# Router scores of a mixture-of-depths stage: from DVE sums over token rows to TensorE products over channel rows

## The chip, the cores and the metric

The kernel runs on one core of a Trainium2 chip, as one program. The metric is the device time in microseconds, the median of three runs. All arithmetic is float32.

The engines by the profile's names: PE (TensorE, matrix products; PEld is its weight load), DVE (VectorE), ACT (ScalarE), POOL (GpSimd), and SP, which issues most DMAs. Each engine takes its instructions in the order in which the program wrote them.

## The reference, cut to what matters

An image of 2 x 256 x 56 x 56 goes through a convolution with local attention, a positional term, six Mamba layers, and then a tail on tokens (2 batches of 3136 tokens of 256 channels). The edit is in the first stage of the tail, a feed-forward layer that only the better half of the tokens of a batch goes through:

```python
t = t + _L2_ffn_ref(_ln_t(t), ...)          # x = _ln_t(t): layer norm of each token
weights = (einsum('bsd,do->bso', x, wr) + br)[..., 0]
_, idx = top_k(weights, k)                  # k = s // 2; the last of them is dropped
h = gelu(sel @ w1 + b1);  y = (h @ w2 + b2) * w_sel
processed = zeros_like(x).at[idx].set(y);  return processed + x
```

The score of a token is one number: the normalised token times the vector `wr`, plus `br`. With mean m and scale r of the token, that is r * (sum(t * wr) - m * sum(wr)) + br, so only sum(t * wr) needs the 256 channels. Behind this stage come an attention step over the two batches and a mixture of eight experts.

## The kernel before, in words

The tail (`tail_phase`, from line 1260) works in groups of 448 tokens, as four rows of 112 (`TK`): seven groups g in each of two batches b. The batch's tokens lie in `t[b]`, 112 partitions by 28 by 256.

The order on each engine is written by a small planner, `Flow`. Each step of work is a Python generator. It takes a tile from a named pool (`yield take("mid")`), waits for a flag (`need`), or says which engine it has just used and for how long by estimate (`yield "PE", 1.1`). The planner resumes generators by these estimates, and the instructions fall into each engine's queue in that order. Another estimate, or another tile, thus moves instructions on all engines. Pools that matter here: `turn` and `mid`, three PSUM tiles each; `chan`, four tiles of channel rows (128 channels by 2 by 448 tokens); `rows`, token rows.

`prepare(b, g)` (line 1404) is the edited generator. It takes the group's channel rows x (for batch 0 from `head[g]`, for batch 1 by a DMA into a `chan` tile), transposes them on PE (L1421) and copies them to `t[b]` on ACT (L1338). `norm` (L1358 to L1367) makes mean and variance on DVE, the root on POOL (L1364), and the two derived columns `up` and `off` on DVE. Then four DVE instructions (L1438) multiply each token row with `wr`, which lies in all 112 partitions, and add it up into `score`; L1444 to L1448 finish the scores. Their product rows go to a `rows` tile that nobody reads; after them ACT writes the normalised rows into the same tile (L1452) and SP stores it to `x_d` (L1457). The generator holds that tile from before L1438.

Batch 0's seven groups run together, with `rest()`, the last step of the Mamba phase: y products (L821, L825) on PE, squares (ACT L776, PE L780), a root (ACT L788, L789), its spread (PE L795), the weighting (DVE L803), an addition on POOL (L845) and a store (SP L846). Four loads of batch 1's channel rows (L1468) stand on SP behind all of these. Batch 1's groups start one after the other: each waits until the one before is scored.

`select(0)` starts when batch 0 is scored. Two radix searches of four rounds each find the threshold: DVE compares and counts (L1534 to L1539), PE adds over the partitions (L1522). Prefix sums follow (L1553, L1554), and `invert` turns places into a list of tokens with one-hots (DVE L1583 to L1591, in `chan` tiles) and products (PE L1596), which ends in `pick` (DVE L1662). POOL gathers the rows by this list (L1396), PE transposes them (L1348), and `dense` runs the two layers (PE L1702, ACT L1708, PE L1716), with `mid` tiles for the first. `select(1)` and `dense(1)` follow.

Of the kernel before, what the change touches and what calls it, by code (L numbers as in the profile page):

```python
# [16 lines left out]
ALU = mybir.AluOpType  # L17
# [4 lines left out]
P = 128  # L22
# [23 lines left out]
TK = 112  # L46
# [13 lines left out]
def chunk(c, n=NT):  # L60
    return slice(c * n, (c + 1) * n)
# [1198 lines left out]
def tail_phase(ctx: ExitStack, tc: tile.TileContext, I, t2_d, out, rest):  # L1260
# [6 lines left out]
    nc = tc.nc  # L1267
# [7 lines left out]
    flow = Flow()  # L1275

    def fixed(shape, name, dtype=F32):
        return cp.tile(shape, dtype, name=name)

    def load(shape, name, src):  # L1280
        t = fixed(shape, name)
        nc.sync.dma_start(t, src)
        return t
# [14 lines left out]
    def take(name):  # L1298
        return "take", name

    def need(*flag):
        return "need", flag
# [6 lines left out]
    wr = load([TK, C], "wr", I["wr_row"].unsqueeze(0).to_broadcast([TK, C]))  # L1309
    earlier = load([TK, TK], "earlier", I["earlier"])  # L1310
    places = load([TK, P], "places", I["count"].unsqueeze(0).to_broadcast([TK, P]))
    token = load([TK, NTK], "token", I["token"])
    wr_sum = fixed([TK, 1], "wr_sum")
    nc.vector.tensor_reduce(wr_sum, wr, AX.X, ALU.add)
    st = [fixed([TK, 6], f"st{n}") for n in range(8)]
# [7 lines left out]
    t, mv, rs, up, off, score = [], [], [], [], [], []  # L1323
# [9 lines left out]
    def four(g):  # L1333
        return slice(4 * g, 4 * g + 4)

    def move(which, dst, src):
        if which == "ACT":
            nc.scalar.copy(dst, src)  # L1338
        else:
            nc.vector.tensor_copy(dst, src)  # L1340
        return which, 0.65
# [11 lines left out]
    def norm(b, g):  # L1353

        s = four(g)
        for n in range(4 * g, 4 * g + 4, 2):
            for i in range(n, n + 2):
                nc.vector.bn_stats(st[i % 8], t[b][:, i, :])  # L1358
            for i in range(n, n + 2):
                nc.vector.bn_aggr(mv[b][:, i, :], st[i % 8])  # L1360
            yield "DVE", 1.1
        nc.vector.tensor_scalar(rs[b][:, s], mv[b][:, s, 1], 1e-5, 0.0, ALU.add, ALU.add)
        yield "DVE", 0.2
        nc.gpsimd.tensor_tensor(rs[b][:, s], rs[b][:, s], half.to_broadcast([TK, 4]), ALU.pow)  # L1364
        yield "POOL", 1.1
        nc.vector.tensor_scalar(up[b][:, s], rs[b][:, s], 1.0, 0.0, ALU.add, ALU.add)
        nc.vector.scalar_tensor_tensor(  # L1367
            off[b][:, s], mv[b][:, s, 0], -1.0, rs[b][:, s], ALU.mult, ALU.mult
        )
# [22 lines left out]
    def rows_of(d, b, g):  # L1392
        return d[b][chunk(g, GT), :].rearrange("(n p) c -> p n c", p=TK)
# [10 lines left out]
    def prepare(b, g):  # L1404

        if b == 0:
            x = head[g]
        else:
            yield need("prepared", 0, NG - 1)
            if g:  # L1410
                yield need("scored", 1, g - 1)
            x = early.pop(g, None)
            if x is None:
                x = yield take("chan")
                nc.sync.dma_start(x, t2_v[b, :, :, chunk(g, GT)])
                yield "wait", 4.0
        for n in range(2):
            ps = yield take("turn")
            for i in range(2):
                for k in range(2):  # L1420
                    nc.tensor.transpose(  # L1421
                        ps[:TK, i * C + k * P : i * C + k * P + P],
                        x[:, k, chunk(2 * n + i, TK)], ident,
                    )
            yield "PE", 0.8
            yield move(
                "ACT", t[b][:, 4 * g + 2 * n : 4 * g + 2 * n + 2, :],
                ps[:TK].rearrange("p (n c) -> p n c", c=C),
            )
            flow.give("turn", ps)  # L1430
        if b:
            flow.give("chan", x)
        yield from norm(b, g)
        s = four(g)
        x = yield take("rows")
        for n in range(0, 4, 2):
            for i in range(4 * g + n, 4 * g + n + 2):
                nc.vector.scalar_tensor_tensor(  # L1438
                    x[:TK, i % 4, :], t[b][:, i, :], 1.0, wr, ALU.mult, ALU.mult,
                    accum_out=score[b][:, i : i + 1],  # L1440
                )
            yield "DVE", 1.1
        sc = score[b][:, s]
        nc.vector.scalar_tensor_tensor(  # L1444
            sc, mv[b][:, s, 0], wr_sum, sc, ALU.mult, ALU.subtract
        )
        nc.vector.scalar_tensor_tensor(sc, sc, -1.0, rs[b][:, s], ALU.mult, ALU.mult)
        nc.vector.tensor_scalar(sc, sc, vec[:TK, V_BR : V_BR + 1], 0.0, ALU.add, ALU.add)  # L1448
        yield "DVE", 0.5
        flow.done("scored", b, g)  # L1450
        for n, i in enumerate(range(4 * g, 4 * g + 4)):
            nc.scalar.activation(  # L1452
                x[:TK, n, :], t[b][:, i, :], AF.Identity,
                scale=rs[b][:, i : i + 1], bias=off[b][:, i : i + 1],
            )
        yield "ACT", 2.4
        nc.sync.dma_start(rows_of(x_d, b, g), x[:TK])  # L1457
        yield "wait", 2.5
        flow.give("rows", x)
        flow.done("prepared", b, g)  # L1460

    flow.start(rest, *[prepare(0, g) for g in range(NG)])
    flow.run()
    cp = pool("tl_const")
# [699 lines left out]
    for b in range(B):  # L2164
        if b:
            flow.start(*[prepare(b, g) for g in range(NG)])
        else:
            flow.start(weights())
        flow.start(select(b), dispatch(b))
# [134 lines left out]
```

## Time and profile before

| what | value |
| --- | --- |
| median of three runs | 8828.61 us (8826.25 to 8833.44) |
| profiled execution | 8834.56 us |
| its span, first to last instruction | 8832.8 us |
| mean granted PE clock | 0.97 |
| busy share: PE, DVE, ACT, POOL | 84%, 89%, 75%, 86% |
| batch 0 prepared | about 7909 to 7956 us of the span |
| L1438, the sums of the scores | 56 instructions, 0.42 us in the median |
| the tail, from its first loads | 7906 to 8833 us |

The busy shares are those of the whole span, of which nine tenths are the convolution and the Mamba layers. The tail is another program in effect, and its stages have limits of their own, so they are read by stretches of the span. In a line of the timeline the first number is the start, the second the length in microseconds; the brackets hold the idle time of that engine before it and what ended it. In a stretch's line each engine has its busy time and, in parentheses, its number of instructions; then come the granted PE clock, the share of the DMA engines, and GB/s.

### The profile page before, as it was taken

The page shows a single profiled execution, that of the slowest core. Times are in us where ns is not written, and L with a number is a line of the kernel's source. Part 1 is how long each engine was busy: PE and PEld are TensorE (multiplying, and loading weights), DVE is VectorE, ACT ScalarE, POOL GpSimd, SP SyncE. Part 2 cuts the span into 40 slices and gives each one's busy share as a digit, 9 for nine tenths or more (in the row PEclk, how much of TensorE's full clock was granted, in tenths as well). Part 3 has the DMA queues.
Part 4 walks back from the last instruction along what each step waited for, and adds up shares of the span by engine and source line. Part 5 has one row for each costly group of instructions (what it writes and reads, how often), then busy time and mean ns, then how long its engine had stood idle before and what let it go on. Part 6 is the DMA issues. An engine that isn't in the chain of part 4 may idle for free.

```text
span 8832.8 us, 106454 instructions
## 1 busy us (share of the span) xinstructions
PE 7458.7 (84%) x32350; PEld 3282.6 (37%) x32350; DVE 7845.9 (89%) x7140; ACT 6659.6 (75%) x15914; POOL 7609.8 (86%) x5255
## 2 busy tenths in 40 slices
PE   9988888888888888888888888888888888867987
PEld 6553333333333333333333333333333333325776
DVE  3339999999999999999999999999999999985664
ACT  1238888888888888888888888888888888863432
POOL 2339999999999999999999999999999999982354
PEclk9999999999999999999999999999999999988988
DMA  2335565655656555556566565556556565543225
GB/s 85 100 116 127 135 135 126 136 131 132 135 132 133 131 132 135 134 133 148 136 137 137 127 133 134 130 133 135 130 133 134 127 138 130 134 118 93 65 72 150
DMA packets 698246, 1118.31 MB, mean 127 GB/s; under 512 B 80060, under 2 KB 675843, under 8 KB 697667
## 3 DMA queue, kind: packets, MB, share of 16 engines
q1 hardware_dynamic: 682888, 1072.49, 52.5%
q0 software_dynamic: 14784, 39.01, 1.5%
q8 instruction: 257, 4.21, 0.2%
q14 instruction: 317, 2.60, 0.1%
HBM read 892.62 MB, written 218.60 MB: 126 GB/s over the span
## 4 chain that ended last, share of the span: by engine, by line
PE 44%; ACT 33%; DVE 13%; issue 6%; DMA 2%; POOL 2%; SPq 0%; ACTq 0%; DVEq 0%; POOLq 0%
ACT da L896 12%; PE mm L683 9%; PE mm L665 8%; PE mm L821 6%; DVE da L934 4%; PE acc L949 4%; DVE x L934 4%; ACT dt L742 2%; DVE x L926 2%; ACT dt L750 2%; ACT hz L695 2%; PE mm L754 2%; ACT dt L749 2%; ACT hz L700 2%; ACT dt L758 1%
## 5 line engine op out<-in xcount | busy, mean ns | idle before, releaser
L913 POOL TENSOR_TENSOR x<-dtur,bc 128x900 f32<-128x900 f32 x2688 | 4717.0, 1793 | 7.8 <-DMA dtur<-dtu_d 7.6
L896 ACT ACTIVATE da<-dtr,am 128x451 f32<-128x451 f32 x5376 | 3417.0, 641 | 323.7 <-DVE x L934 153.9
L934 DVE TENSOR_TENSOR_SCAN da<-da,x 128x902 f32<-128x902 f32 x1512 | 3040.1, 2031 | 97.5 <-ACT da L896 70.9
L934 DVE TENSOR_TENSOR_SCAN x<-da,x 128x902 f32<-128x902 f32 x1176 | 2341.5, 2018 | 46.6 <-ACT da L896 38.2
L926 POOL TENSOR_TENSOR x<-x,bc 128x896 f32<-128x896 f32 x1176 | 2080.1, 1784 | 80.9 <-DVE x L934 80.9
L926 DVE TENSOR_TENSOR x<-da,bc 128x896 f32<-128x896 f32 x1512 | 1604.1, 1075 | 20.5 <-ACT state L922 9.0
L949 PE MATMUL acc<-x,sum_w 128*32 128x448 f32 x10752 | 1382.5, 568 | 59.2 <-DVE x L926 33.9
L683 PE MATMUL mm<-u,w_cv 128*128 128x448 f32 x2656 | 1093.8, 554 | 67.0 <-ACT tail L678 56.9
L665 PE MATMUL mm<-xn,w_z 128*128 128x448 f32 x1328 | 587.0, 564 | 196.5 <-ACT dt L758 116.7
L683 PEld LDWEIGHTS mm<-u,w_cv 128*128 128x128 f32 x2656 | 478.6, 190 | 677.7 <-issue 375.9
L665 PE MATMUL mm<-xn,w_u 128*128 128x448 f32 x1328 | 579.0, 558 | 121.2 <-ACT hz L695 111.8
L821 PE MATMUL mm<-hz,w_out 128*128 128x448 f32 x1344 | 553.7, 555 | 107.9 <-ACT tail L678 56.3
L949 PEld LDWEIGHTS acc<-x,sum_w 128*32 128x32 f32 x10752 | 266.2, 111 | 966.7 <-issue 732.7
L754 PE MATMUL mm<-dt,mb_ident 128*128 128x448 f32 x666 | 342.1, 595 | 257.6 <-ACT state L922 139.4
L737 PE MATMUL mm<-xd,w_dt 128*128 128x448 f32 x664 | 339.2, 592 | 217.2 <-ACT dtu L745 128.6
L912 ACT COPY x<-state 128x2 f32<-128x2 f32 x2688 | 437.1, 187 | 0.1
L665 PEld LDWEIGHTS mm<-xn,w_z 128*128 128x128 f32 x1328 | 225.4, 189 | 564.5 <-ACT dt L758 236.4
L665 PEld LDWEIGHTS mm<-xn,w_u 128*128 128x128 f32 x1328 | 231.5, 189 | 457.8 <-ACT hz L695 223.1
L821 PEld LDWEIGHTS mm<-hz,w_out 128*128 128x128 f32 x1344 | 243.3, 191 | 417.9 <-issue 189.2
L766 POOL TENSOR_TENSOR dtu<-dt,hz 128x448 f32<-128x448 f32 x336 | 330.9, 985 | 76.6 <-PE mm L755 76.6
L695 ACT ACTIVATE hz<-mm,vec 128x448 f32<-128x448 f32 x332 | 209.2, 630 | 243.1 <-PE mm L683 238.8
L944 PE MATMUL acc<-hz,w_sk 128*128 128x448 f32 x672 | 347.0, 600 | 31.7 <-DVE hz L963 31.7
(377 smaller groups left out, 9536.9 us busy)
## 6 DMA issues: line engine op xcount, KB each, us to landing
dtr<-dt_d SPq DMA_DIRECT2D x1344, 224.0 KB, 4.4
dtur<-dtu_d SPq DMA_DIRECT2D x1344, 224.0 KB, 6.7
bc<-bc_d SPq DMA_DIRECT2D x336, 448.0 KB, 7.8
dt_d<-dt SPq DMA_DIRECT2D x336, 224.0 KB, 6.2
dtu_d<-dtu SPq DMA_DIRECT2D x336, 224.0 KB, 2.0
rows<-r_d SPq DMA_DIRECT2D x28, 448.0 KB, 7.9
xg<-in_x SPq DMA_DIRECT2D x26, 448.0 KB, 8.9
bm<-in_edge SPq DMA_DIRECT2D x16, 539.0 KB, 4.6
```

Source lines behind the costliest of these rows:

```text
L665: nc.tensor.matmul(ps, lhsT=w[:, k, chunk(d, P)], rhs=Q["xn"][:, k, :], start=(k == 0), stop=(k == 1),)
L683: nc.tensor.matmul(ps, lhsT=w_cv[:, 4 * d + k, :], rhs=M["u", d][:, k : k + T], start=(k == 0), stop=(k == 3),)
L695: nc.scalar.activation(hz(j)[:, d, :], M["mm"], AF.Identity, bias=layer_of(j + 1)["cb"][:, d : d + 1])
L754: nc.tensor.matmul(ps, lhsT=ident, rhs=M["dt"][:, d, :], start=True, stop=False)
L821: nc.tensor.matmul(ps, lhsT=layer_of(j - 1)["w_out"][:, d, chunk(k, P)], rhs=gated(j - 1)[:, d, :], start=(d == 0), stop=False,)
L896: nc.scalar.activation(D[i][:, chunk(g, R)], dtr[:, 2 * pr + g, :], AF.Exp, scale=L["am"][:, col : col + 1],)
L912: nc.scalar.copy(x[:, :, 0:1], states(i))
L913: nc.gpsimd.tensor_tensor(x[:, :, 1:], Q[k][1][:, 2 * pr : 2 * pr + 2, :], wide(Q["bc"][:, ng, :]), ALU.mult)
L926: engine.tensor_tensor(both(X[i])[:, :, 1 : T + 1], both(h)[:, :, 1 : T + 1], wide(QS[j]["bc"][:, 4 + ng, :T]), ALU.mult,)
L934: nc.vector.tensor_tensor_scan(h, D[i], X[i], 0.0, ALU.mult, ALU.add)
L944: nc.tensor.matmul(acc[0][:, :T], lhsT=L["w_sk"][:, k, :], rhs=Q["hz"][:, k, :], start=True, stop=False,)
L949: nc.tensor.matmul(acc[0][chunk(g, HD), :T], lhsT=sum_w, rhs=both(X[i - 1 + g // 2])[:, g % 2, 1 : T + 1], start=False, stop=(ng == 3), ti ...
```

## The change

The sum over channels is taken on PE from the channel rows, before they are given back, instead of on DVE from the token rows. `wr` is loaded a second time, as two columns of 128 channels. For each row of 112 tokens two products (the two halves of the channels) add up one column of a `mid` tile, eight products a group; L1444 reads it from there. The `mid` tile is held from the products until L1444, through `norm`. A `chan` tile is held until the products are issued. The `rows` tile is taken only after the scores. The planner's estimates change with it: 1.1 for PE is new, two of 1.1 for DVE are gone.

```diff
+    wr_col = fixed([P, 2], "wr_col")
+    nc.sync.dma_start(wr_col, I["wr_row"].rearrange("(k p) -> p k", p=P))
...
             flow.give("turn", ps)
+        raw = yield take("mid")
+        for i in range(4):
+            for k in range(2):
+                nc.tensor.matmul(
+                    raw[:TK, i : i + 1], lhsT=x[:, k, chunk(i, TK)], rhs=wr_col[:, k : k + 1],
+                    start=(k == 0), stop=(k == 1),
+                )
+        yield "PE", 1.1
         if b:
             flow.give("chan", x)
         yield from norm(b, g)
         s = four(g)
-        x = yield take("rows")
-        for n in range(0, 4, 2):
-            for i in range(4 * g + n, 4 * g + n + 2):
-                nc.vector.scalar_tensor_tensor(
-                    x[:TK, i % 4, :], t[b][:, i, :], 1.0, wr, ALU.mult, ALU.mult,
-                    accum_out=score[b][:, i : i + 1],
-                )
-            yield "DVE", 1.1
         sc = score[b][:, s]
         nc.vector.scalar_tensor_tensor(
-            sc, mv[b][:, s, 0], wr_sum, sc, ALU.mult, ALU.subtract
-        )
+            sc, mv[b][:, s, 0], wr_sum, raw[:TK, :4], ALU.mult, ALU.subtract
+        )
+        flow.give("mid", raw)
         nc.vector.scalar_tensor_tensor(sc, sc, -1.0, rs[b][:, s], ALU.mult, ALU.mult)
         nc.vector.tensor_scalar(sc, sc, vec[:TK, V_BR : V_BR + 1], 0.0, ALU.add, ALU.add)
         yield "DVE", 0.5
         flow.done("scored", b, g)
+        x = yield take("rows")
```

## The prediction

> **What bounds the kernel now.** I read the page first, then the busy time by stretch around the edited stage, the edited line by itself, the timeline and the chain of waits there. Times of the walk are given less 7900 us.
>
> ```profile
> span 8832.8 us, 106454 instructions
> ```
>
> ```profile
> 7931.00:7938.00 7.00, 5.19 (x42) 4.28 (x40) 7.00 (x43) 5.95 (x13) 2.45 (x3) 1.00 0.00 0
> 7938.00:7956.00 18.00, 0.00 (x0) 0.00 (x0) 17.44 (x95) 12.10 (x24) 7.37 (x10) 0.51 0.55 167
> 7956.00:7998.00 42.00, 12.66 (x53) 10.34 (x54) 32.48 (x152) 7.89 (x15) 2.02 (x2) 0.50 0.59 193
> 7998.00:8011.00 13.00, 12.28 (x64) 12.07 (x64) 8.15 (x33) 3.25 (x6) 1.67 (x1) 0.50 0.24 71
> 8020.00:8060.00 40.00, 40.00 (x168) 27.61 (x169) 18.07 (x83) 19.14 (x34) 11.84 (x12) 0.96 0.32 94
> ```
>
> The columns are PE, weight loads, DVE, ACT, POOL, then the granted clock. Nothing before 7908 is touched. Batch 0 is scored between 7920 and 7956, and there DVE is full. `select(0)` runs from 7956 to 8011, a relay of short DVE and PE steps. From 8020 PE is full, 40.00 of 40 us, so DVE time taken away there is worth nothing and PE time added costs its full length. Last, the clock: it falls to half at 38.2 and stays there to 8022, also in 7998 to 8011, where PE is busy 12.28 of 13 us.
>
> ```profile
> L1438 DVE SCALAR_TENSOR_TENSOR rows<-t,wr x56: 412/418/1635, 7932.2 to 8057.2; 112x256 f32<-112x256 f32 x56
> ```
>
> ```profile
> 537.49 3.15 PE L780 MATMUL early<-mb_mean_w,sq 128*112 128x1 f32 x16 [3.66 <-ACT sq L776]
> ```
>
> ```profile
> 8171.54 1.64 PE L1789 MATMUL mid<-vec,query 128*112 128x1 f32 x16
> ```
>
> The first line is what goes: 56 DVE sums, 0.35 us from start to start where they stand in a row (7932.17, 7932.51, 7932.86 in the timeline). The two others are the shape that comes (eight 128x112 by 128x1 products, recorded as 16): 3.1 us at half clock and, its first weight load left out, 1.5 us at full.
>
> ```profile
> 7930.41 3.04 POOL L1364 TENSOR_TENSOR rs<-rs,tl_half 112x4 f32<-112x4 f32 x3 [19.99 <-DVE rs L1362]
> ...
> 7935.50 1.14 PE L795 MATMUL mm<-mb_ident,rss 112*128 112x112 f32 x8
> ...
> 7939.59 1.24 DVE L803 SCALAR_TENSOR_TENSOR o<-res,normf,mm 128x448 f32<-128x448 f32 x2
> 7940.91 2.07 POOL L845 TENSOR_TENSOR hz<-hz,o 128x896 f32<-128x896 f32 x1 [1.02 <-DVE o L803]
> ```
>
> ```profile
> 7956.61 4.98 DMA chan<-t_d
> 7961.64 1.12 PE turn L1421 x4
> ...
> 8003.69 2.80 PE mid L1596 x14
> 8006.48 1.77 PE turn L1421 x8
> 8008.26 2.46 PE mid L1596 x14
> 8010.75 0.17 DVE pick L1662
> ```
>
> The four timeline lines are the last step of `rest()`, threaded through batch 0: its L795 feeds L803, that feeds POOL's L845. The chain shows what follows batch 0: SP may issue the loads of batch 1 only after the last `x_d` store, which waits for ACT's last L1452 (ends 56.2); then the relay; then `pick`, after which rows are gathered and PE's full stretch starts.
>
> **The change part by part.** Removed: 56 x 0.35 = 19.6 us of DVE, half in each batch. In batch 1 the last three groups' share lies beside a full PE and was worth nothing. Added: 14 x 16 recorded products, 1.5 or 3.1 us a group. The written order of the engines moves too, and it decides. I lay the new order out with these durations.
>
> *Batch 0.* PE leaves `rest()`'s second L825 at 31.4. The new order then has products of g0, transposes, g1, transposes, g2, transposes (3 x 1.5 + 3 x 0.5): 37.4. L780 follows, during which the clock falls (38.2): 39.6. Transposes at half clock 1.1: 40.7. Then the products of g3, g4 and g5 stand ahead of L795: 3 x 3.1, so 50.0, and L795 ends about 52.0 against 36.6. They find their PSUM tiles free in time (DVE's first three scores end by 37.8).
> DVE has L803 ahead of the `rs` step of g3 in the new order, so DVE stands still at it from about 41.3, and all behind it waits: L803 ends 53.2. POOL has L845 ahead of the L1364 steps of g3 to g6; before, g3's came ahead of it and DVE fed the others in time: L845 ends 55.3, then L1364 of g3, g4, g5 at 1.0 us each. ACT's L1452 needs these: four groups from 56.6 at 2.07 us each end at 64.9, against 56.2. So +8.7 us, though DVE has 28 x 0.35 = 9.8 us less to do. The bounds are the clock: at full clock until L795, the same walk gives +2; falling 2.3 us earlier, +12. I take the moment this execution shows.
>
> *The relay.* Batch 1's products now stand in PE's queue between the relay's own L1522 sums. In the first radix the product follows round 1 (3.1 us, the next round is ready after 2.0, and DVE puts g0's statistics there): +0.4. In the second, transposes and product (1.1 + 3.1) stand between rounds 5 and 6; the round's result comes 5.3 us after round 5 began against 3.35: +1.95. Four sums leave DVE before `sm_eq`, one score comes ahead of it: -0.5. One statistics pair is now ahead of the one-hots: +0.85. Sum +2.7 (bounds -1.5, all four groups' DVE sums saved and products covered, to +4).
> *The inversion.* Before, from 7997.85 to 8010.75: 12.9 us. Now 4 x 2.7 of L1596, 2 x 1.1 of transposes, 3.1 of product, 0.4 for one-hots behind a POOL step: 16.5. So +3.6 (bounds 1 to 4).
> *Gathers.* Four are issued in a row now, without L1364 between: -1.0 (bounds -1.5 to 0).
> *Before the first dense layer.* A fifth product stands between the two halves of the gathered rows' transposes, PE in order and idle-fed: +3.1 (1.5 at full clock).
> *PE's full stretch.* Two more products at 1.5, less two groups of transposes (0.44 each) that now come before it: +2.1 (bounds 2 to 3).
>
> From about 8250 on every engine's written order is the same as before, and PE is the chain up to 8130, so the delay is handed on; the one hole there, behind 28 activations of ACT at 8130 to 8144, sits at the same place of the new order.
>
> Costed at nothing: the load of `wr_col` on SP (the 12 KB `token` load ahead of it lands in 5.1 us; the first user is 14 us later; behind it on SP wait the store L846 and the load L835, whose data POOL's L845 needs 20 us later). If it landed 15 us late, it would cost those microseconds at 31.4. Three `x_d` stores that move ahead of SP's second L846 are issued before that store's data exists. The PSUM operand of L1444: 112x4, 0.22 us either way.
>
> Sum: 8.7 + 2.7 + 3.6 - 1.0 + 3.1 + 2.1 = 19.2 us; by the low and high bounds 3.5 to 26. The profiled execution took 8834.56 us, 1.8 over its span and 6 over the median of runs, 8828.61. The delay is added to each: span 8852, median **8848**.
>
> [...]
>
> **The rivals.** *The clock stays up*, because the added products keep PE active. For it: PE would be busy where it now idles 25 us. Against it: the rows above. Then batch 0 costs +2, the relay -1.5; L1596 and L1522 run in half their time (-5), the transposes too (-1); the products of the inversion and before dense cost 1.5 each, gathers -1.0, the first L1702 -1.1, the stretch +2.1: together -2.5, **8826**. It decides if the profile shows the clock at 1.0 after 7945.
> *DVE's time comes out whole*: only if PE's added work is covered everywhere, and the rest of `rest()` does not hold DVE. Batch 0 -9.8 alone gives 8819; with all of batch 1's, -19.6, **8809**. Against it: PE's position of L795 and full PE after 8020.
> *Dense waits for PSUM as well*: `dense` takes its accumulators from the same three `mid` tiles, and a product's tile is held through DVE's statistics and POOL's L1364, which for g4 is queued behind six gathers (1.3 each). If DVE's score of g4 comes 12 us after the first dense product or later, L1702 stands; about another 12 us, **8860**. My walk has it free some 5 us early.
> That the scores would not be summed on PE is excluded: the new instructions are in its order.
>
> **How the numbers follow.** Forecast 0.62, with 8839 to 8858 as its own range; clock 0.17; whole DVE gain 0.08; PSUM wait 0.13. A measurement can tell 0.2%, 17.7 us, from no change: the border is 8846.3. Of the forecast 0.47 lies above it and 0.15 below; with the PSUM wait slower is 0.60. The clock case, that 0.15 and 0.03 of the DVE case make same 0.35; the rest of the DVE case is faster, 0.05. The range, 8824 to 8862, takes in the clock case at the bottom and the PSUM wait at the top; it leaves out the DVE case and the outermost ends of the bounds.
>
> **What would show it.** L795 after 7945 with L803 and L845 right behind it; DVE idle ahead of L803 for 5 us or more; ACT's last L1452 of batch 0 after 7960; the added products near 3 us a group before 8025 and 1.5 after; `pick` 12 to 17 us later than 8010.75; the rest shifted whole. I am wrong if `pick` is earlier than 8012, if the clock is 1.0 in the relay, or if the shift at 8130 is not that at the end.

## The result, and the profile after

| | kernel before | changed kernel |
| --- | --- | --- |
| median | 8833.44 us (8826.25 to 8843.87) | 8856.83 us (8851.5 to 8869.86) |
| profiled span | 8832.8 us | 8854.1 us |

The ratio is 1.0026 (95% interval 1.0018 to 1.0035): the change costs 23.4 us, or 21.3 us between the two profiled spans. Predicted were 8848 us, and 19.2 us for the delay. DVE has 17.9 us less to do over the span (7828.0 against 7845.9 us busy), and none of it reaches the end.

The page and the busy time by stretch, in the columns of the prediction:

```profile
span 8854.1 us, 106814 instructions
```

```profile
7931.00:7938.00 7.00, 7.00 (x52) 6.53 (x51) 4.19 (x26) 2.65 (x4) 2.11 (x3) 0.79 0.00 0
7938.00:7956.00 18.00, 16.83 (x88) 16.56 (x88) 5.18 (x21) 7.43 (x16) 0.00 (x0) 0.50 0.26 77
7956.00:7998.00 42.00, 16.47 (x81) 15.56 (x81) 28.44 (x131) 12.28 (x24) 9.07 (x12) 0.50 0.70 220
8011.00:8035.00 24.00, 19.58 (x101) 18.48 (x101) 8.49 (x33) 7.84 (x14) 8.00 (x8) 0.50 0.34 104
8060.00:8100.00 40.00, 39.74 (x181) 28.13 (x179) 22.07 (x85) 9.72 (x17) 1.05 (x1) 1.00 0.12 35
```

The second line is the place to look at. Before, PE was idle there and DVE full (17.44 of 18 us); now PE is busy for 16.83 us, at half clock, and DVE for 5.18. The work did move, but DVE's place was not taken by earlier work: it waits. The timeline of batch 0 shows for what:

```profile
7931.84 1.64 PE L1436 MATMUL mid<-wr_col,h 128*112 128x1 f32 x16
7933.80 1.93 PE L1436 MATMUL mid<-wr_col,h 128*112 128x1 f32 x16
7936.46 3.01 PE L1436 MATMUL mid<-wr_col,h 128*112 128x1 f32 x16
7940.21 3.01 PE L780 MATMUL mm<-mb_mean_w,sq 128*112 128x1 f32 x16
7943.96 8.98 PE L1436 MATMUL mid<-wr_col,h 128*112 128x1 f32 x48
7952.80 2.03 PE L795 MATMUL mm<-mb_ident,rss 112*128 112x112 f32 x8
7954.87 1.27 DVE L803 SCALAR_TENSOR_TENSOR o<-res,normf,mm 128x448 f32<-128x448 f32 x2 [11.24 <-PE mm L795]
7956.22 2.07 POOL L845 TENSOR_TENSOR hz<-hz,o 128x896 f32<-128x896 f32 x1 [18.62 <-DVE rs L1364]
7958.25 2.98 POOL L1366 TENSOR_TENSOR rs<-rs,tl_half 112x4 f32<-112x4 f32 x3
7959.63 7.97 ACT L1456 ACTIVATE rows<-t,off,rs 112x256 f32<-112x256 f32 x16 [11.46 <-DVE off L1369]
```

(Line numbers behind L1310 have moved: L1438 is gone, L1436 is the products, L1364 became L1366 on POOL, L1452 became L1456, L1522 L1526, L1596 L1600, L1662 L1666, L1396 L1398, L1348 L1350, L1702 L1706, L1716 L1720.) L795 ends at 54.83 behind the products of three groups, 18.2 us later than before. DVE's L803 has stood 11.24 us for it, POOL's L845 follows, then the roots that ACT needs, and ACT writes its last four groups without a break until 67.60 (less 7900). Before, that was 56.23. The rest of the way to PE's full stretch:

```profile
8025.79 0.17 DVE L1666 CAST pick<-mid 112x14 uint32<-112x14 f32 x1 [3.11 <-PE mid L1600]
...
8030.47 0.99 POOL L1398 DMA_INDIRECT rows<-x_d,pick  x1 [0.30 <-issue]
...
8033.40 3.01 PE L1436 MATMUL mid<-wr_col,chan 128*112 128x1 f32 x16
...
8037.05 1.73 PE L1706 MATMUL mid<-chan,wide 128*128 128x448 f32 x2
```

`pick` is 15.0 us later than before, the first dense product 15.3 (8021.74 before). From there to the hole behind ACT's 28 activations, PE is the chain in both kernels. These are the two stretches, before and after, from the first dense product to the last PE work ahead of the hole:

```profile
8021.74:8135.90 114.16, 113.65 (x513) 81.44 (x512) 49.72 (x199) 37.56 (x69) 21.68 (x23) 0.99 0.18 54
```

```profile
8037.05:8157.66 120.61, 118.63 (x546) 84.72 (x544) 45.24 (x172) 35.12 (x66) 22.16 (x22) 0.98 0.16 46
```

The stretch is 6.4 us longer. The lines of PE in the stretch after say by what:

```profile
L1350 PE MATMUL turn<-tl_ident,rows 112*128 112x112 f32 x38 | 6.1, 269 | 1.5 <-DMA rows<-x_d,pick 1.5
L1436 PE MATMUL mid<-wr_col,chan 128*112 128x1 f32 x32 | 3.3, 233 | 0.0
L1423 PE MATMUL turn<-tl_ident,chan 128*112 128x128 f32 x16 | 2.4, 272 | 0.0
```

Two groups of products are 3.3 us; six more recorded transposes of gathered rows 1.3 (6.1 against 4.8); fewer channel transposes -1.0 (2.4 against 3.4); the two dense products 0.9 more (110.8 against 109.9); other small sums 0.4; and PE is idle 1.98 us instead of 0.51, 1.5 of them waiting for gathered rows (0.5 before). Together 6.4. The clock rises 3.8 us after the first dense product in this profile and 1.8 us after it before, which at half speed makes about the 0.9.

### The profile page after: what moved, and what is told of

The parts are those of the page before. It is cut to its first block, busy times and chain, and to the rows that moved or that the text cites. A ratio compares the mean times of both kernels' runs of the same rounds, so it can differ in the third digit from the quotient of the medians.

```text
span 8854.1 us, 106814 instructions
## 1 busy us (share of the span) xinstructions
PE 7508.7 (85%) x32574; PEld 3323.1 (38%) x32574; DVE 7828.0 (88%) x7028; ACT 6659.9 (75%) x15914; POOL 7607.6 (86%) x5255
## 4 chain that ended last, share of the span: by engine, by line
PE 43%; ACT 33%; DVE 12%; issue 6%; POOL 2%; DMA 2%; SPq 0%; ACTq 0%; POOLq 0%; DVEq 0%
ACT da L896 12%; PE mm L683 9%; PE mm L665 8%; PE mm L821 6%; DVE da L934 4%; PE acc L949 4%; DVE x L934 4%; ACT dt L742 2%; DVE x L926 2%; ACT dt L750 2%; ACT hz L695 2%; PE mm L754 2%; ACT dt L749 2%; ACT hz L700 2%; ACT dt L758 1%
```

## Experiments

The later runs are from chips on which the kernel before takes 8863 to 8878 us; each ratio is against the kernel before on the same chip. There are three of them: batch0_by_pe, batch1_by_pe, no_sums and late_products are from one, before_again from another, and the other seven from the third. Stages are compared by four marks, counted from the start of the mixer's last L825 in the same profile: the relay's first sum, `pick`, the first dense product, and the start of the last product of the second dense matrix ahead of the hole, before which all kernels have the same dense work.

| kernel | first sum | pick | first dense | last ahead of hole | ratio (95% interval) |
| --- | --- | --- | --- | --- | --- |
| before | 32.4 | 79.8 | 90.8 | 203.0 | |
| before_again | 33.2 | 80.5 | 91.5 | 203.5 | 0.9997 (0.9988 to 1.0007) |
| changed | 43.5 | 94.3 | 105.6 | 224.3 | 1.0026 (1.0018 to 1.0035) |
| changed_again | 42.8 | 93.6 | 104.9 | 224.4 | 1.0042 (1.0029 to 1.0056) |
| batch0_by_pe | 44.2 | 91.6 | 102.6 | 215.6 | 1.0012 (1.0002 to 1.0021) |
| batch1_by_pe | 32.6 | 83.4 | 94.7 | 213.6 | 1.0027 (1.0017 to 1.0037) |
| batch1_first_four | 32.3 | 83.1 | 91.6 | 204.0 | 1.0009 (1.0000 to 1.0019) |
| no_sums | 27.7 | 75.7 | 87.0 | 198.5 | 1.0003 (0.9994 to 1.0013) |
| late_products | 35.5 | 86.3 | 97.6 | 216.3 | 1.0032 (1.0020 to 1.0045) |
| wide_fills | 44.4 | 95.2 | 106.5 | 225.0 | 1.0043 (1.0028 to 1.0058) |
| before_early_loads | 28.7 | 75.9 | 86.9 | 199.3 | 1.0002 (0.9993 to 1.0011) |
| split_early_loads | 23.3 | 74.9 | 85.8 | 198.1 | 0.9994 (0.9985 to 1.0003) |
| before_warm_clock | 32.8 | 80.8 | 91.8 | 203.7 | 1.0003 (0.9994 to 1.0012) |
| split_early_warm | 23.3 | 80.8 | 91.8 | 204.6 | 0.9999 (0.9990 to 1.0008) |

**One batch at a time.** The switch is one condition around the products and DVE's sums of the kernel before; it is `b == 0` in batch0_by_pe, `b == 1` in batch1_by_pe, and `b == 1 and g < 4` in batch1_first_four:

```diff
+        by_pe = b == 0
+        if by_pe:
+            raw = yield take("mid")
...
+        else:
+            x = yield take("rows")
+            for n in range(0, 4, 2):
...
```

> Only batch 0's scores are summed on TensorE, batch 1 keeps its DVE sums. Theory (two separate losses: the order of batch 0, and TensorE work in batch 1): batch 0 as in the changed kernel, L795 ends near 7955 and ACT's last rows at 7967 to 7968, so +11 us; the relay, the inversion and the first dense layer as in the kernel before, only shifted. Span about 8844 us (+10 to +12.5 over before). Rival (batch 0's delay is swallowed by the relay, and most of the loss is batch 1's products on a full TensorE): span within 4 us of before.

> Only batch 1's scores are summed on TensorE. Theory: batch 0 ends as in the kernel before (rows at 7956, DVE full to there), the relay about +1, the inversion +2 to +3, the products before and in the first dense layer +6 to +7: span about 8843 us (+8 to +12). Rival (only the two products in the full stretch count, the rest is covered by the relay's waits): +3 us, 8836.

> Batch 0 and the last three groups of batch 1 keep DVE's sums; only groups 0 to 3 of batch 1, whose products lie in the relay and the inversion, go by TensorE. Theory (the product ahead of the first dense layer and the two in TensorE's full stretch cost their own length and what moves with them, 6 to 7 us in all): up to the first pick as with all of batch 1 on TensorE (pick 83.4 us after the mixer's last L825, against 79.75), first dense product at 92 to 93 instead of 94.7, and the stretch from there to the end of the hole behind ACT's 28 activations 123 to 125 us long instead of 129.5. Rival (the stretch is longer because its order is another, with or without the products): 128 or more.

Batch 0 alone: first sum 11.8 us later than in the kernel before, first dense product 11.8, then the last mark 12.6 against the first profile of before (12.2 against the second); by time 10.7 us. Batch 1 alone: batch 0 untouched, `pick` 3.6 later, first dense product 3.9, last mark 10.2 to 10.6. So there are two losses, each there without the other, and their sum at the last mark, 22 to 23 us, is 1 to 2 more than both together lose (20.9 to 21.4). The rival of batch 0, that the relay swallows its delay, falls; so does the rival of batch 1 (+3 us). By time, though, batch 1 alone costs 24 us (15 to 33), more than its marks and more than the expected 8 to 12; that rest comes up again under the controls.

With only the first four groups of batch 1 on PE, `pick` is as late as with all seven (83.1 against 83.4), but the first dense product is at 91.6 and the last mark at 204.0, within 1.0 us of the kernel before. The stretch between them is 112.4 us, as before (112.3), against 118.9 with all seven; to the end of the hole, as the expectation counts it, 123.2 us against 129.6. The three last groups thus carry nearly all of batch 1's loss: 3.1 us at the first dense product and 6.5 in the full stretch, of which the products themselves are 3.3. The first four cost 0.8 us in sum: relay and inversion lose 3.4 us, and 2.5 come back between `pick` and the first dense product (8.5 us against 11.0), where POOL issues the gathers in a row and channel transposes no longer stand ahead of it. The expectation's rival, that the order alone makes the stretch longer, falls.

**The place of the products in batch 0.** The products of groups 3 to 6 are written only once L795 is; the flag `spread` is set when `rest()` has written its last one:

```diff
+        late = b == 0 and g >= 3
+        if not late:
+            raw = yield from products()
         yield from norm(b, g)
+        if late:
+            yield need("spread")
+            raw = yield from products()
```

> The changed kernel, but batch 0's products of groups 3 to 6 are written behind the mixer's last L795 instead of ahead of it; the same work otherwise. Theory (their place in TensorE's order is what batch 0 loses by): L795 ends near 7946 instead of 7954.8, L803 and L845 right behind, ACT's last rows near 7959 instead of 7967.6; batch 1's loss of 10 us stays: span about 8845 us (8842 to 8848). Rival (TensorE's added time counts wherever it stands): as the changed kernel, 8854.

The timeline of this run, with PE's products on L1437:

```profile
7944.19 3.01 PE L780 MATMUL mm<-mb_mean_w,sq 128*112 128x1 f32 x16
7947.94 1.90 PE L795 MATMUL mm<-mb_ident,rss 112*128 112x112 f32 x8
7949.63 3.01 PE L1437 MATMUL mid<-wr_col,h 128*112 128x1 f32 x16
7949.88 1.27 DVE L803 SCALAR_TENSOR_TENSOR o<-res,normf,mm 128x448 f32<-128x448 f32 x2 [2.33 <-PE mm L795]
7951.23 2.07 POOL L845 TENSOR_TENSOR hz<-hz,o 128x896 f32<-128x896 f32 x1 [2.60 <-DVE o L803]
```

The products of groups 3, 4 and 5 that came ahead of L795 now come behind it, and DVE's wait for L795 is 2.33 us instead of 11.24. ACT's last rows end 28.1 us after the mixer's last L825, against 36.1 in the changed kernel and 25.3 in the kernel before. The last mark is 8.1 us earlier than in changed_again on the same work. At ACT's last rows three quarters of batch 0's loss is therefore the place of nine microseconds of products in PE's queue, not the products. In time no gain can be seen (1.0032, with an interval that overlaps those of the changed kernel); the stages carry this reading.

**What DVE's time is worth.**

```diff
-        sc = score[b][:, s]
-        nc.vector.scalar_tensor_tensor(sc, mv[b][:, s, 0], wr_sum, raw[:TK, :4], ALU.mult, ALU.subtract)
+        sc = score[b][:, s]
+        nc.vector.tensor_scalar(sc, mv[b][:, s, 0], wr_sum, 0.0, ALU.mult, ALU.add)
```

> Left out: the weighted sums of both batches, on either engine (a score keeps only its mean term). What taking the work off DVE is worth when nothing is put in its place. Theory: L795 stays where it was (7936.6), DVE has 9.8 us less in batch 0 but POOL's L845 and ACT set the pace, so ACT's last rows come 4 to 6 us earlier; the relay gains 1 to 2; full TensorE gains nothing: span 8824 to 8828 us (-5 to -9). Rival (DVE's time comes out whole): -20 us, 8813. Second rival (DVE was hidden): within 1 us of before.

ACT's last rows come 5.2 us earlier (20.0 against 25.3 after the last L825), as expected. Then the gain stops growing: 4.7 us at the first sum, 3.8 at the first dense product, 4.6 to 5.0 at the last mark, and in time nothing can be told from zero (1.0003, 0.9994 to 1.0013). That is the low end of the expected 5 to 9 us, and 20 is far off. What DVE's 19.6 us were worth at the last mark, with nothing put in their place, was under 5. What holds batch 0 then was not taken apart; DVE's statistics are still first in its chain, with POOL's root and ACT's rows behind them.

**The clock.** Two wide products of no use ahead of each of the groups 3 to 6 in batch 0:

```diff
         raw = yield take("mid")
+        if b == 0 and g > 2:
+            for i in range(2):
+                nc.tensor.matmul(raw[:, 16:464], lhsT=ident, rhs=x[:, i, :GT], start=True, stop=True)
```

> The changed kernel with two 128x448 products of no use put ahead of each raw product group 3 to 6 of batch 0. At half clock the two take 3 us a group, at full 1.5. Theory (what keeps the clock at half is that 128x1 products and short transposes stream few columns, busy or not): the clock comes to 1.0 within some 5 us of the first fill, the raw products after it take 1.6 instead of 3.0, and L795 ends near 56 us against 54.8, at most 3 later. Rival (the clock follows busy time over a longer stretch, whatever the shape): the clock stays at 0.50, a group takes 6 us, L795 ends 9 us later than in the changed kernel.

PE's timeline (fills on L1436, products on L1439) and the granted clock, the third figure from the end in the stretch lines:

```profile
7942.42 3.01 PE L780 MATMUL mm<-mb_mean_w,sq 128*112 128x1 f32 x16
7945.30 1.08 PE L1423 MATMUL turn<-tl_ident,h 128*112 128x128 f32 x4
7946.17 2.67 PE L1436 MATMUL mid<-h,tl_ident 128*128 128x448 f32 x4
7948.68 1.64 PE L1439 MATMUL mid<-wr_col,h 128*112 128x1 f32 x16
7950.18 1.75 PE L1436 MATMUL mid<-h,tl_ident 128*128 128x448 f32 x4
```

```profile
7938.00:7946.00 8.00, 8.00 (x44) 8.00 (x44) 5.83 (x29) 3.64 (x9) 1.01 (x1) 0.50 0.01 2
7946.00:7950.00 4.00, 4.00 (x21) 2.68 (x19) 0.00 (x0) 4.00 (x9) 0.00 (x0) 0.73 0.66 190
7950.00:7954.00 4.00, 4.00 (x26) 2.98 (x26) 0.00 (x0) 0.39 (x1) 0.00 (x0) 1.00 0.51 154
```

In all three stretches PE is busy the whole time. With narrow products the clock is 0.50 through 8.00 busy us of 8.00; 2.0 us after the first fill began it is full, and the same products take 1.64 us instead of 3.01. L795 ends 23.5 us after the last L825, against 23.4 in the changed kernel (22.6 in changed_again), with twelve more recorded fills ahead of it. Busy time alone thus does not decide here; the clock came up with the wide products. Whether it is their columns, or that weight loads fill all of the time with narrow products (8.00 of 8.00 us) and less of it in the stretch with the first wide pair (2.68 of 4.00), these runs don't part.

Does a full clock then help the stages behind? Fills of no use behind the relay's sums and between the groups of the inversion:

```diff
     def total(n, src, ps):
         nc.tensor.matmul(ps[:TK, :n], lhsT=ones, rhs=src, start=True, stop=True)
+        warm(2)
...
+    def warm(n, src=vec):
+        for ps in warmth:
+            for _ in range(n):
+                nc.tensor.matmul(
+                    ps[:TK, :GT], lhsT=ident[:TK, :TK], rhs=src[:TK, :1].to_broadcast([TK, GT]),
+                    start=True, stop=True,
+                )
...
+            warm(1 if q else 2, row)
             for i in range(7):
```

> The kernel before, with TensorE products of no use, 112x448, put behind the relay's sums (two each), behind the prefix sums (one each) and between the inversion's groups (two, then one each). Theory (the clock comes up with some 3 us of wide products and narrow ones then run in half the time): clock 1.0 from the second round on, the inversion's four groups 1.4 instead of 2.7 us each, relay 1 to 3 us shorter, from the last prefix to pick 4 to 5 us shorter: first dense product 84 to 86 us after the mixer's last L825 instead of 90.74. Rival (the gaps of the relay let the clock fall again, and the fills stand in the way of the sums): clock at 0.5 to 0.7 there, first dense product at 91 to 95.

The first stretch is the relay, the second the inversion:

```profile
7970.00:7990.00 20.00, 16.01 (x56) 7.24 (x55) 17.36 (x81) 4.83 (x10) 1.78 (x2) 1.00 0.66 207
8000.00:8013.00 13.00, 13.00 (x65) 9.59 (x63) 8.92 (x34) 3.25 (x6) 1.67 (x1) 0.65 0.24 72
```

```profile
8001.73 1.70 PE L1609 MATMUL mid<-chan,chan 112*112 112x14 f32 x14
8003.28 0.99 PE L1531 MATMUL mid<-sm_lo,tl_ident 112*112 112x448 f32 x2
8004.10 1.45 PE L1609 MATMUL mid<-chan,chan 112*112 112x14 f32 x14
8005.41 1.60 PE L1531 MATMUL mid<-sm_lo,tl_ident 112*112 112x448 f32 x2
8006.80 2.73 PE L1609 MATMUL mid<-chan,chan 112*112 112x14 f32 x14
...
8012.54 1.46 PE L1609 MATMUL mid<-chan,chan 112*112 112x14 f32 x14
```

In the relay the clock is 1.00, and the relay is as long as ever: first to eighth sum 21.9 us against 21.8 before, since DVE sets it (17.36 of 20 us busy). In the inversion three of the four groups do run in 1.45 to 1.70 us; for the other (2.73) the clock has fallen again with PE busy throughout, and what they save goes to the fills. First dense product at 91.8 against 90.8: half of the theory (the clock) holds, and the gain does not come. By the mark the rival was right, by the clock in the relay the theory.

**A version that might gain.** The relay's first sum stands behind batch 1's transposes in PE's order, and these wait for loads that stand on SP behind batch 0's stores. The loads move ahead; in the second kernel batch 0's groups 3 to 6 also go by PE, behind L795, and batch 1 stays on DVE (the last line of the diff is this kernel's alone):

```diff
+    for g in range(4):
+        early[g] = flow.free["chan"].popleft()
+        nc.sync.dma_start(early[g], t2_v[1, :, :, chunk(g, GT)])
     flow.start(rest, *[prepare(0, g) for g in range(NG)])
...
-    for g in range(4):
-        early[g] = flow.free["chan"].popleft()
-        nc.sync.dma_start(early[g], t2_v[1, :, :, chunk(g, GT)])
...
+        by_pe = b == 0 and g >= 3
```

> The kernel before, with the four first loads of batch 1 issued on SP ahead of batch 0's stores instead of behind the last of them. Theory (the relay's first sum waits for these loads through the transposes ahead of it in TensorE's order; its DVE operand lay ready 3.7 us earlier): first round 3.7 us earlier, all later stages shifted, span -3 to -4. Rival (DVE or ACT is just as late): -1 or less.

> A version meant to gain: batch 0 keeps DVE's sums for groups 0 to 2, groups 3 to 6 go by TensorE but behind the mixer's last L795; batch 1 is all DVE's; the early loads of batch 1 as in the other run. Theory (DVE time is worth something only in batch 0 after 7938, TensorE has nothing to do there, and the position ahead of L795 was the harm): L795 where the kernel before has it, ACT's last rows 4 to 5 us earlier, the relay's first round 7 to 9 us earlier than in the kernel before, every later stage alike: span -6 to -9, ratio 0.9990 to 0.9994. Rival (the products at half clock are late: the last score waits for four groups of 3.05 us): -3.7 us, no more than the loads alone.

The loads alone bring the first sum 3.7 us forward and the first dense product 3.9, as expected; 3.8 are left at the last mark, and none can be seen in the time (1.0002). The split brings the first sum to 23.3, 9.1 earlier, and by the second sum only 4.9 are left (31.1 against 36.0 us). The timeline between the two sums:

```profile
7947.37 11.90 ACT L1477 ACTIVATE rows<-t,off,rs 112x256 f32<-112x256 f32 x24 [8.07 <-issue]
...
7955.59 0.56 PE L1553 MATMUL mid<-reached,ones 112*112 112x15 f32 x2 [3.17 <-DVE reached L1570]
7959.18 1.04 ACT L1340 COPY t<-turn 112x512 f32<-112x512 f32 x2
7959.77 0.75 DVE L1360 BATCH_NORM_STATS2 st<-t 112x6 f32<-112x256 f32 x2 [4.24 <-ACT t L1340]
```

DVE has batch 1's statistics ahead of the second round, these need ACT's copy, and ACT is in its rows until 59.3 (less 7900); why these start only at 47.4 the view doesn't show. ACT's rows end later than in the kernel before (27.0 against 25.3 after the last L825), not 4 to 5 us earlier: the expectation had DVE as the only bound. At the last mark 4.9 us are gained, 1.2 more than by the loads alone, in time 0.9994 (0.9985 to 1.0003). It has the lowest ratio of all versions and is well below the changed kernel; that it beats the kernel before is not shown.

> The best of the runs so far (batch 0's groups 3 to 6 by TensorE behind L795, batch 1 by DVE, early loads), with the fills in the relay and the inversion. Theory: the two gains add, first dense product at 78 to 81 us after the mixer's last L825 (85.7 without the fills, 90.74 in the kernel before), time 10 to 12 us under before, ratio 0.9986 to 0.9990. Rival: as without the fills, 85 to 87, ratio 0.9994.

With the fills the first sum stays at 23.3 and the first dense product falls back to 91.8: the fills cost all of it. The rival is right and was still too kind.

**Controls.** Both kernels again, unchanged:

> The changed kernel once more, as a control beside the other three. Runs of one chip differ from runs of another by tens of us in the mixture-of-experts part, where ACT stands 5 to 13 us with nothing in the profile that releases it, so stages are compared from the last L825 of the mixer on. Theory (the loss is laid down before 250 us after that point): relay's first round 11 us later than in the kernel before, first dense product 15 later, ratio 1.0026 as before, within its interval. Rival (the tail decides, by where the code lies): the same stage times, but a ratio that is off by 0.1% or more.

> The kernel before once more, for its profile on the chip of the later runs. There the changed kernel's profile has 110 us of waits behind 7950 whose releaser the profile does not know, 45 of them ACT's, and on the first chip none. Theory (these waits belong to that chip's tail whatever the kernel, and only their sum differs): the kernel before has 60 to 110 us of them too, its stages up to the hole behind ACT's 28 activations agree with the first chip's profile within 1 us (relay's first round 32.4, first pick 79.75, first dense product 90.74 after the mixer's last L825). Rival (the change brings them): under 30 us of them.

At all marks both agree with their first profile within 1 us: the loss of some 21 us is in place at the last mark on either chip. The ratio of changed_again, 1.0042, is off by more than the 0.1% that its rival names, but its interval overlaps that of the first, so a difference in time is not shown. Behind the last mark the chips differ. These two lines are ACT's in changed_again, behind the hole:

```profile
8164.53 0.63 ACT L1712 ACTIVATE hid<-mid,vec 128x448 f32<-128x448 f32 x1 [5.72 <-PE mid L1706]
8178.09 0.63 ACT L1712 ACTIVATE hid<-mid,vec 128x448 f32<-128x448 f32 x1 [12.92 <-remote]
```

ACT stands 12.92 us, and the view names no releaser on this core. Such waits add up, over all engines behind 7950, to none in the first two profiles and to 51 us in before_again, between the 60 to 110 of its theory and the under 30 of its rival. But before_again is from another chip than changed_again (110), so these two cannot be compared. On the chip of changed_again, before_early_loads, with no product of the change, has 88; so most of them do not come from the change. All four later kernels with the whole of batch 1 on PE have 92 to 110, the other kernels of the same two chips 63 to 88. They lie one over another, so their sum is no loss of time.

In time the same four kernels (batch1_by_pe, changed_again, late_products, wide_fills) lose 14 to 16 us more by their ratios than at the last mark; for the other later kernels the difference lies between 3 us less and 8 more, and for the changed kernel on the first chip it is 2. One ratio is good to some 9 to 13 us, but the four agree. So on the later chips the change seems to cost something behind the last mark too, where none of its products stand; the cause is open. This is why ratios here tell less than marks.

## Why the prediction was right, by its own steps

The forecast and its sign were right, with 8848 us against 8856.83; 4.8 of the 8.8 us between them are the kernel before itself, whose nine runs give 8833.44 where the three that the forecast started from gave 8828.61. The terms were less right: two were too small, by 7.0 us together, and the others too large, by 4.9. That the sum is off by only 2.1 is in good part luck.

| term | predicted (bounds) | measured in the two profiles |
| --- | --- | --- |
| batch 0: ACT's last L1452 | +8.7 (2 to 12) | +11.4 (67.60 against 56.23) |
| the relay | +2.7 (-1.5 to 4) | +1.4 (11.4 becomes 12.8 at the first L1596) |
| the inversion | +3.6 (1 to 4) | +2.3 (15.2 against 12.9 us) |
| gathers, `pick` to the fourth | -1.0 (-1.5 to 0) | -1.6 (4.7 against 6.3 us) |
| product ahead of dense | +3.1 | +1.9 (6.6 against 4.7 us from the fourth gather) |
| full stretch | +2.1 (2 to 3) | +6.4 |
| behind the hole | 0 | -0.5 |
| sum | +19.2 | +21.3 |

**Batch 0.** The mechanism is as written: L795 behind the products of g3, g4, g5, then L803, L845, POOL's roots and ACT, link by link, and late_products shows that the place does three quarters of it. The size failed at the moment of the clock. I took 38.2, where it fell in the kernel before; in the profile after it fell at 35.0, as two stretches show:

```profile
7934.90:7938.00 3.10, 3.10 (x19) 3.10 (x19) 2.07 (x14) 0.59 (x1) 1.01 (x1) 0.51 0.00 0
7934.00:7934.90 0.90, 0.90 (x11) 0.90 (x11) 0.90 (x5) 0.59 (x1) 0.00 (x0) 1.00 0.00 0
```

That is 3.0 us after the last wide product (L825, which ends near 32.0), with PE busy throughout. So g2's products and L780 ran at half speed too (3.01 us each), and L795 ended 2.8 us later than forecast, 0.5 of which were there at L825 already, ahead of any product. The fall came 3.2 us earlier than taken, the 2.3 of the text's upper bound was too little, and its +12 still covers the 11.4. One execution could not have told the moment: in the four profiles with the changed kernel's batch 0 up to L795 the clock falls 2.9 to 3.8 us after the last L825, in those with the order of the kernel before 3.4 to 9.8 (6.7 in the one that the forecast used, 3.4 in before_again). Around this fall the clock was full for 13.65 us and then at half for 85.33 in before, and full for 10.24 and at half for 105.81 in after.

**The relay.** Of the two rounds that a product delays, the cost was over-counted: the first sum is 11.6 us late and the fifth 11.3, so the first product costs nothing; with the second it is 12.8 at the sixth sum, 1.5 more instead of 1.95.

**The inversion.** Each piece is a little shorter on the chain than I took it (the product 2.80 for 3.1, a group of transposes 0.92 for 1.1), and the wait of 0.4 for one-hots behind POOL did not come.

**Gathers and the product ahead of dense.** The gathers gain a little more than their bound, as POOL has nothing between them. The product is on the chain with 2.81 us, and 0.85 us of channel transposes that stood there before are gone, which the term had left out.

**The full stretch.** Here the step failed, and its bounds with it: two products less two groups of transposes was too short a list. These two come to 2.3 (3.3 less 1.0). What was left out is more idle time (1.5, of which 1.0 for gathered rows), more transposes of gathered rows in the stretch (1.3), the later rise of the clock (0.9) and other small sums (0.4). batch1_first_four, whose stretch is as long as before, puts the whole of it on the last three groups.

**The rivals.** "The clock stays up" did not come (0.50 from 7938 to 8035), and its price was wrong as well: before_warm_clock has the relay at full clock and gains nothing, for DVE sets it. "DVE's time comes out whole" would have been 20 us; without any sums it is under 5. "Dense waits for PSUM as well" did not come at dense, where PE shows no wait for a `mid` tile; one such wait is in batch 0, where g6's products stood 4.89 us for DVE's score of an earlier group, beside the chain.

**The signs.** L795 after 7945, DVE idle 11.24 us ahead of L803, ACT's last rows after 7960, `pick` 15.0 us later and the same shift from the hole (21.8) to the end (21.3) are as named. The products took 3.0 us up to 8036, a little past the 8025 of the text.

## What to carry to other kernels

Work that is moved to an idle engine is paid by its place in that engine's queue: read what stands behind it and who waits for that, since nine microseconds of products in front of one small product cost eight. Before an engine is relieved, leave its work out once and look at the marks behind: here all of DVE's 19.6 us were worth under 5. And add up the whole list of what a new order brings into a full stretch, not the added instructions alone.

## What the runs showed of the hardware that was not expected

- The granted clock fell while PE was busy without a gap: it went to half 3.0 us after the last 128x448 product in the changed kernel's profile, with 3.10 of 3.10 us busy behind it, and 8.00 of 8.00 busy us of 128x1 products and 128-column transposes stayed at 0.50 in wide_fills.
- In wide_fills it was full 2.0 us after the first of two 128x448 products began, and 128x1 products behind them took 1.64 us a group instead of 3.01; with another such pair 4.0 and again 3.1 us later it stayed there (1.00 from 7950 to 7958), and it fell 3.4 us after the third pair (0.55 over 7958 to 7962).
- The moment of the fall was not the same in two profiles of one kernel: 6.7 us after the end of the last L825 in before, 3.4 us in before_again.
- On the later chips engines stood up to 12.9 us in waits for which the view names no releaser on the core; the first two profiles have none.
